# Layer 3 of a four-layer convolution kernel: q and k projections as single products under an account that carries room over, and the second head pair's scores first

## The chip, the cores and the metric

The kernel runs on one core of one Trainium2 chip. The metric is device time in microseconds. Three runs of the kernel before took 3479.43, 3482.70 and 3486.44 us, so its median is 3482.7 us. A profile of one further execution, which took 3485.36 us, is what the sections below read.

The engines are called as in the profile: PE is TensorE's matrix multiplier and PEld its weight load, DVE is VectorE, ACT is ScalarE, POOL is GpSimd, SP issues nearly all DMAs. Each engine runs its own instructions in the order in which the program gives them.

## The reference, cut to what matters

The input `x` has shape (4, 256, 48, 48). Four layers follow each other, each of the form `x = x + layer(_gn(x))` with a group norm over 32 groups. Layers 0 to 2 are convolutions; the change leaves them alone. Layer 3 is an attention without softmax, in three windows:

```python
q = jnp.einsum('bchw,oc->bohw', x, Wq).reshape(b * h, d, Hh, Ww)
k = jnp.einsum('bchw,oc->bohw', x, Wk).reshape(b * h, d, Hh, Ww)
v = jnp.einsum('bchw,oc->bohw', x, Wv).reshape(b * h, d, Hh, Ww)
q = jax.nn.sigmoid(q)
k = jax.nn.sigmoid(k)
v = v / jnp.maximum(jnp.linalg.norm(v, axis=1, keepdims=True), 1e-12)
...
for w in WINDOWS:                      # 1, 2, 4
    ws = Hh // w
    wk = _box(Ik, ws, Hh, Ww)          # sums of k over a window around each place
    wkv = _box(Ikv, ws, Hh, Ww)        # the same of k times v
    attn = jnp.einsum('bdhw,bdfhw->bfhw', q, wkv)
    norm = jnp.einsum('bdhw,bdhw->bhw', q, wk)
    attn = attn / (norm[:, None] + 1e-06)
    outs.append(attn.reshape(b, C, Hh, Ww))
o = jnp.concatenate(outs, axis=1)
return jnp.einsum('bchw,oc->bohw', o, Wout) + bout[None, :, None, None]
```

There are 8 heads of 32 channels. A window's sum of k times v, multiplied by q, is the same as the sum over the window's places of (q times k) times v, and this is how the kernel computes it.

## The kernel before, in words

**Blocks and steps of layer 3.** A block is one batch (4), one half of the channels (2, four heads each) and one block of 8 rows (6): 48 blocks in the list `order`. A block's keys come in tiles of 8 rows by 16 columns, `tiles_of` (line 2003): 12, 15 or 18 tiles for a block, near rows and far rows in turn. Each tile of each block is one step of the loop at line 2201; there are 720 steps, 180 for each batch, 90 for each half of the channels.

**What a step does.** It issues the scores of its tile (line 2206): for each of the two head pairs `pr` one PSUM tile `s` of two banks and two matmuls of 32 rows, which stand on different row groups of the array. `unseen` (line 1855) adds a large negative penalty with one matmul per head, pair 0 first. `masked` (line 1875) turns scores into masked sums `sm`. In a tile whose rows all lie in the widest window, ACT takes the edges of the second pair (`widest`) while DVE takes the middle window of the first pair (`middle`), and then ACT the edges of the first pair and DVE the middle of the second (lines 1943 to 1947). In a tile at row distance 3, ACT takes the first pair and DVE the second. In near tiles POOL multiplies the narrowest window's mask on. Two steps later (`LAG`, line 84) `sums` (line 1980) multiplies `sm` by the values into the three accumulators. The pool of `s` tiles has two buffers, so the next step's scores wait for this step's masks.

**The side jobs.** Everything else of layer 3 is a generator in the list `active`: the projections q, k, v of the next batch (`qk`, line 423; `v`, line 457), the window sums of k (`k_sums`, line 1621), the norms (`norms`, line 1663), the states (`state`, line 1761), the preparation of outputs (`prepare`, line 2017) and the output product (`finish`, line 2050). `advance` (line 302) runs once at the end of each step and lets each job go on to its next `yield`, in the order of the list: norms and `finish_all` were started first, so they come ahead of the projections of the next batch. A group of 8 rows gives eight projection jobs (a load, four of q and k, three of v), and `paced(following, 2)` starts one of them every two steps.

**The account.** The variable `spare` holds the nanoseconds of PE time that a step may give to side jobs. At the end of a step it becomes `min(spare, 0.0) + time` (line 306): a debt is carried on, room that was not used is dropped. `time` is `900.0 + mask_time - sums_time`, at least 500 (lines 2226 to 2229); `mask_time` (line 2170) prices the masks of this step, `sums_time` (line 2184) the sums that PE does in it. A job takes its turn with `turn(cost)` or `bank(steps, cost)` (lines 329 to 342), which wait until `spare` is at least 0.6 of its cost and then subtract the cost. `product_time` (line 349) prices a matmul at 1.67 ns a column, so one of 384 columns at 641 ns. An `advance()` without a time, as in `until` (line 318), grants `ALL`, which is without limit: that is how the loop forces a result that it needs at once, and how the first projections run beside the convolutions.

**The one bank.** `s` has four of the eight PSUM banks, the three accumulators have one each, and `ps_m` has the last one. All side products use it. `bank(steps, ...)` closes it for so many steps; with `HOLD` (1000) it is closed until `keep_bank(1)`. A q or k product is 256 channels deep, so it is two matmuls of 128 rows into the same tile; both are issued in one turn at a cost of 1,283 ns (line 430).

**The v chain.** After a group's third v product, POOL squares, DVE reduces, and POOL takes four steps of a Newton iteration for the reciprocal root (lines 500 to 505), one per step of the loop; a step later DVE multiplies `vt` by it (line 506). The norms of a block of rows put up to twelve operations of 128x384 on `nhi` to POOL within about four steps (lines 1705 to 1714).

## Time and profile before

| what | value |
|---|---|
| median of three runs | 3482.7 us |
| time of the profiled execution | 3485.36 us |
| its span, first to last instruction | 3483.6 us |
| first score of layer 3 | 1,389 us |
| busy in the span: PE, DVE, ACT, POOL | 3059.6, 1994.0, 1041.5, 1532.2 us |
| mean granted clock of TensorE | 0.951 |
| scores `s<-qs,ks` | 5760 records, mean 506 ns |
| sums `acc<-sm,vs` | 14976 records, mean 306 ns |
| q and k products in layer 3 | 148 and 148 records of a mean of 522 and 520 ns |
| wait of PE's scores for DVE and for ACT, layer 3 | 61.6 and 60.4 us |
| wait of PE's sums for POOL | 48.5 us |

A matmul in float32 leaves two records, so one q or k product leaves four. In a page of the profile, the slices cut the span into 40 equal parts of 87 us; each digit is the busy share in tenths. A row of the timeline gives start and length in us, engine, operation, what is written and read, and in brackets the idle time of the engine before it with what ended that. A row of the waits gives total, number and longest. The engine whose wait ends last in a step sets when the next step begins.

### The profile page before, as it was taken

The page shows a single profiled execution, that of the slowest core. Times are in us where ns is not written, and L with a number is a line of the kernel's source. Part 1 is how long each engine was busy: PE and PEld are TensorE (multiplying, and loading weights), DVE is VectorE, ACT ScalarE, POOL GpSimd, SP SyncE. Part 2 cuts the span into 40 slices and gives each one's busy share as a digit, 9 for nine tenths or more (in the row PEclk, how much of TensorE's full clock was granted, in tenths as well). Part 3 has the DMA queues.
Part 4 walks back from the last instruction along what each step waited for, and adds up shares of the span by engine and source line. Part 5 has one row for each costly group of instructions (what it writes and reads, how often), then busy time and mean ns, then how long its engine had stood idle before and what let it go on. Part 6 is the DMA issues. An engine that isn't in the chain of part 4 may idle for free.

```text
span 3483.6 us, 78045 instructions
## 1 busy us (share of the span) xinstructions
PE 3059.6 (88%) x31634; PEld 1931.6 (55%) x31634; DVE 1994.0 (57%) x3595; ACT 1041.5 (30%) x2782; POOL 1532.2 (44%) x2548
## 2 busy tenths in 40 slices
PE   3579999999899788888789988889998999989998
PEld 2467776767768557444344544444554444545544
DVE  7986488568657336465564445554456554444444
ACT  0012111211111423444323433433344433334432
POOL 0000030021011214587886678786557786534443
PEclk9799899999999899999899999999999999999999
DMA  7745413413322422344554444354423454401221
GB/s 256 236 139 174 141 63 122 154 54 129 120 94 85 138 89 98 120 132 145 164 144 129 127 137 146 116 158 134 124 81 119 130 150 122 114 29 52 81 63 56
DMA packets 373052, 423.34 MB, mean 122 GB/s; under 512 B 129076, under 2 KB 328532, under 8 KB 371540
## 3 DMA queue, kind: packets, MB, share of 16 engines
q1 hardware_dynamic: 371491, 416.32, 38.3%
q8 instruction: 249, 4.08, 0.5%
q0 software_dynamic: 144, 1.24, 0.2%
q14 instruction: 112, 0.91, 0.1%
q10 hardware_dynamic: 1056, 0.79, 0.1%
HBM read 288.24 MB, written 131.25 MB: 120 GB/s over the span
## 4 chain that ended last, share of the span: by engine, by line
PE 56%; POOL 12%; DVE 11%; ACT 4%; issue 3%; DMA 3%; SPq 1%; ACTq 0%; POOLq 0%; DVEq 0%
PE s L208 15%; PE cv L208 14%; PE acc L208 11%; PE out_ps L208 6%; PE proj_ps L208 4%; DVE sm L208 3%; POOL nhi L208 3%; ACT sm L208 3%; POOL sm L208 3%; POOL pt L208 2%; PE ap L208 2%; POOL vu L208 1%; DVE l2v L208 1%; DVE v L208 1%; DVE k L208 1%
## 5 line engine op out<-in xcount | busy, mean ns | idle before, releaser
L208 DVE TENSOR_TENSOR sm<-s,masks 128x432 f32<-128x432 f32 (+8 forms) x1152 | 634.4, 578 | 627.8 <-PE s L208 582.0
L208 POOL TENSOR_TENSOR sm<-sm,masks 128x336 f32<-128x336 f32 (+8 forms) x768 | 606.1, 809 | 662.6 <-DVE sm L208 656.2
L208 ACT ACTIVATE sm<-s 128x128 f32<-128x128 f32 (+3 forms) x1680 | 559.1, 361 | 1030.9 <-PE s L208 820.9
L208 PE MATMUL s<-qs,ks 32*128 32x320 f32 (+3 forms) x5760 | 664.5, 506 | 127.9 <-DVE sm L208 61.6
L208 PE MATMUL acc<-sm,vs 128*32 128x64 f32 (+13 forms) x14976 | 681.8, 306 | 48.6 <-POOL sm L208 48.5
L208 PE MATMUL cv<-vx,wt 128*128 128x288 f32 x2080 | 560.1, 425 | 93.2 <-DVE vx L208 52.6
L208 PEld LDWEIGHTS acc<-sm,vs 128*32 128x32 f32 x14976 | 347.9, 110 | 384.5 <-issue 258.4
L208 PEld LDWEIGHTS cv<-vx,wt 128*128 128x128 f32 x2080 | 402.5, 198 | 214.5 <-issue 56.7
L208 PEld LDWEIGHTS s<-qs,ks 32*128 32x128 f32 x5760 | 264.4, 187 | 422.9 <-ACT sm L208 172.4
L208 POOL MEMSET v<- 128x16 f32 (+1 forms) x120 | 18.5, 215 | 727.7 <-DVE vx L208 634.5
L208 PE MATMUL cv<-v,wl 128*128 128x384 f32 x1152 | 225.1, 355 | 25.7 <-DVE x L208 10.6
L208 DVE TENSOR_SCALAR sm<-s 128x672 f32<-128x672 f32 (+1 forms) x144 | 118.6, 824 | 202.8 <-PE s L208 198.1
L208 PEld LDWEIGHTS cv<-v,wl 128*128 128x128 f32 x1152 | 214.3, 194 | 36.0 <-issue 15.9
L208 PE MATMUL s<-masks 24*128 24x128 bf16 (+4 forms) x2880 | 217.7, 236 | 0.0
L208 POOL TENSOR_TENSOR pt<-pt 128x144 f32<-128x144 f32 x336 | 188.5, 561 | 23.0
L208 POOL TENSOR_TENSOR v<-l2v,v 128x384 fp32r<-128x384 f32 x96 | 109.0, 1163 | 120.2 <-ACT v L208 111.3
L208 POOL TENSOR_TENSOR nhi<-nhi,nq 128x384 f32<-128x384 f32 x144 | 144.8, 1033 | 0.2
L208 PE MATMUL cv<-pad,wl 128*128 128x384 bf16 x864 | 143.1, 327 | 0.0
L208 PE MATMUL out_ps<-o,wout_sb 128*128 128x384 f32 x288 | 130.2, 534 | 3.6 <-DVE res L208 2.8
L208 PEld LDWEIGHTS <-masks 24*128 24x128 bf16 x2880 | 101.5, 95 | 53.9 <-issue 3.5
L208 PEld LDWEIGHTS <-wl 128*128 128x128 bf16 x864 | 83.8, 97 | 59.3 <-issue 0.7
L208 PE MATMUL out_ps<-stage,wout_sb 128*128 128x384 f32 x288 | 116.4, 486 | 0.0
(176 smaller groups left out, 3568.6 us busy)
## 6 DMA issues: line engine op xcount, KB each, us to landing
wt<-wt SPq DMA_DIRECT2D x48, 768.0 KB
kb_d<-pt SPq DMA_DIRECT2D x48, 576.0 KB
rc<-r_d SPq DMA_DIRECT2D x192, 144.0 KB
nhi<-kb_d SPq DMA_DIRECT2D x120, 192.0 KB
nlo<-kb_d SPq DMA_DIRECT2D x88, 192.0 KB
o_d<-stage SPq DMA_DIRECT2D x24, 576.0 KB
o<-o_d SPq DMA_DIRECT2D x24, 576.0 KB
wl<-wl_d SPq DMA_DIRECT2D x16, 768.0 KB
```

Source lines behind the costliest of these rows:

```text
L208: return lambda *args, **kwargs: self.tc.keep_in_program_order(op(*args, **kwargs))
```

## The change

Four edits, all in the planning of layer 3:

1. The account carries unused room, up to `MOST` = 600 ns, and a step's room is `450.0 + mask_time - sums_time`, at least 300, in place of 900 and 500.
2. A q or k product takes its turn for each of its two matmuls at 641 ns. It holds the bank from the first one to the second, as `norms` and `finish` do.
3. `keep_bank(1)` opens the bank one step after the second matmul.
4. The scores of a step are issued for head pair 1 and then for pair 0. The list `ss` is turned back, so that penalties and masks come in the order of before.

```diff
-        spare = ALL if time is None else min(spare, 0.0) + time
+        spare = ALL if time is None else min(spare, MOST) + time
...
-    ALL = 1e6
+    ALL, MOST = 1e6, 600.0
...
             yield from take("kt")
-            yield from bank(1, NCT * product_time(NB))
+            yield from bank(HOLD, product_time(NB))
             ps = self.ps_tile()[:, 0:NB]
             for ct in range(NCT):
+                if ct > 0:
+                    yield from turn(product_time(NB))
                 pe.matmul(
...
+            keep_bank(1)
             self.used(g)
...
-                ss = [blocks[i].scores(pr, a, c) for pr in range(NPR)]
+                ss = [blocks[i].scores(pr, a, c) for pr in reversed(range(NPR))][::-1]
...
-                time = 900.0 + mask_time(*stream[n][:3]) - sums_time(*stream[n - LAG][:4])
-            advance(max(time, 500.0))
+                time = 450.0 + mask_time(*stream[n][:3]) - sums_time(*stream[n - LAG][:4])
+            advance(max(time, 300.0))
```

## The prediction

> **What bounds the kernel now.** I read the page first: its busy line, its slices, then the 87 us windows of layer 3, the waits, and two stretches of the timeline.

> ```profile
> PE 3059.6 (88%) x31634; PEld 1931.6 (55%) x31634; DVE 1994.0 (57%) x3595; ACT 1041.5 (30%) x2782; POOL 1532.2 (44%) x2548
> ...
> PE   3579999999899788888789988889998999989998
> ...
> POOL 0000030021011214587886678786557786534443
> PEclk9799899999999899999899999999999999999999
> ```

> Layer 3 runs from 1,389 us (slice 16) to the end: some 2,090 us, 720 steps. TensorE is its busiest engine, but POOL is close wherever projections and norms run. Three windows (us, then PE, PEld, DVE, ACT and POOL busy, granted clock, DMA):

> ```profile
> 1651.00:1738.00 87.00, 64.93 (x821) 34.19 (x819) 46.52 (x76) 28.57 (x84) 72.34 (x126) 0.85 0.59 176
> 1912.00:1999.00 87.00, 84.53 (x1145) 44.79 (x1141) 38.95 (x68) 35.57 (x105) 51.78 (x70) 1.00 0.42 124
> 3043.00:3130.00 87.00, 78.55 (x1236) 43.69 (x1234) 39.25 (x69) 30.82 (x93) 35.51 (x59) 1.00 0.09 29
> ```

> With POOL at 72 of 87 us, PE falls to 65 and the clock to 0.85; with POOL at 52, PE has 84.5 and the full clock. The waits of layer 3 (total, times, longest) say who holds whom:

> ```profile
> DVE vt L208 <- POOL vr L208: 104.7, 18, 12.1
> PE s L208 <- DVE sm L208: 61.6, 92, 9.5
> PE s L208 <- ACT sm L208: 60.4, 110, 4.0
> PE acc L208 <- POOL sm L208: 48.5, 36, 5.3
> ```

> The first is a jam. VectorE's scaling of v stands ahead of the next mask and waits for POOL's reciprocal roots, which stand behind the norms' `nhi` work:

> ```profile
> 1674.50 1.94 POOL L208 TENSOR_TENSOR nhi<-nhi,nlo 128x384 f32<-128x384 f32 x2
> 1678.26 1.09 PE L208 MATMUL acc<-sm,vs 128*32 128x132 f32 x6 [5.28 <-POOL sm L208]
> 1678.82 2.90 POOL L208 TENSOR_TENSOR nhi<-nhi,nq 128x384 f32<-128x384 f32 x3
> 1682.87 0.96 DVE L208 TENSOR_TENSOR vt<-vt,vr 128x768 f32<-128x768 f32 x1 [12.07 <-POOL vr L208]
> 1684.82 1.53 PE L208 MATMUL s<-qs,ks 32*128 32x320 f32 x8 [3.97 <-ACT sm L208]
> ```

> PE stands for 9 us; the scores then take 1.53 instead of 0.82 us, at half clock.

> I sorted the matmuls of layer 3 by step (from one step's first score to the next one's). 328 steps with no side product have a median of 2.07 us; 139 with about 0.54 us of them (at the account's prices) 2.56; 195 with about 1.28 us 3.26. Side work is thus almost additive: a step hides only some 0.1 to 0.4 us. Above 2.07 + 0.93 per us of side work, 42 long steps lose 170 us: 82 in batch 0, 51 in batch 1, 32 in batch 2, 5 in batch 3, which projects nothing. The half-clock stretches there (145 us, 72 us lost) are mostly inside that sum.

> [...] eight score records, 506 ns each on average, span 0.82 us[...]

> **The change part by part.**

> *Convolution stages.* The first q, k, v run there with unlimited room, so both halves of a product go in one turn: nothing moves before 1,389 us.

> *Room.* Evaluating mask time minus sums time for all steps gives a mean of 292 ns. Room is now max(900+d, 500), mean 1,223 ns, the unused part dropped; then max(450+d, 300), mean 793, with up to 600 carried. Demand per batch: 24 q/k at 1,283 ns, 18 v at 855, 24 state uses (12 states, a transpose and a product each) at 641, 12 norm turns and 36 output turns at 1,283: 123 us, 684 ns a step. Supply falls from 220 to 143 us: enough, but used to 86% instead of 56%.

> *q and k.* 74 products of layer 3 (296 records of four) are cut in two. No matmul is added. Split in two steps, each half finds its own slack: in steps of like d, 0.54 us of side work cost 0.37 where 1.28 cost 1.14, so a second step hides about 0.15 us more. With 1,393 at best after an idle step (600 + 793) both halves still go together (1,026 is needed), else not; I take 45 split: 45 x 0.15 = -7 us; bounds 0 and -30 (74 x 0.4). Behind a split move the sigmoid (490 ns on ACT), for k the copy (0.51), and two or one DMA issues (0.4 us each on SP), past the norms' loads in SP's order; their readers come steps later, which hides it; uncovered it is one step, 2 to 3 us, per product that somebody waits for.

> *The one bank.* q/k hold it about 1.6 steps instead of 1. Bank steps per batch, mine: q/k 24 to 38, v 18, states 24, norms 18 to 21, outputs 60 to 74 (a second-half turn finds 793 a step, not 1,223). Sum 144 to 175 of 180. Outputs and norms stand first in the list of jobs, projections last. Now q, k and v come in runs of ten steps in a row (steps 9 to 18 have 1.28 or 0.85 us in each), at over 1 us a step; with 0.79 a run of ten spreads over some fifteen.

> *Where the jam goes.* In batch 0 the norms run every 16 to 17 steps (copies at steps 57, 74, 91, 107) and the v chains too (scalings at 55, 71, 88, 103), since a group's eight jobs start two steps apart. A norm's `nhi` work (six products at 1.03 us and up to six differences at 0.97) thus falls on the four steps of the roots each time: near the worst phase. Later v's move off it, and one step of lag drains about 3 us of POOL's queue. A v chain late by 3 to 5 steps escapes most of a 9 us jam. But norms get about one step longer each and may meet other chains. I take a gain of a sixth of the 170 us: -28. Bounds: -80 (batch 0's jams gone) and +50 (batches 1 and 2 as bad as batch 0).

> *Second pair first.* Masks and penalties keep their order; only four matmuls swap. The timeline of two steps with no side work:

> ```profile
> 3161.12 0.93 PE L208 MATMUL s<-qs,ks 32*128 32x384 f32 x8 [0.43 <-DVE sm L208]
> 3162.13 1.52 DVE L208 TENSOR_TENSOR sm<-s,masks 128x624 f32<-128x624 f32 x2 [1.07 <-PE s L208]
> 3162.97 0.45 ACT L208 ACTIVATE sm<-s 128x128 f32<-128x128 f32 x2 [0.29 <-DVE sm L208]
> 3163.47 1.15 PE L208 MATMUL s<-qs,ks 32*128 32x384 f32 x8 [0.43 <-ACT sm L208]
> ```

> The first score waits once for VectorE, once for ACT: the first to be issued gets the buffer that comes free first. The other came 0.2 us later (1.15 instead of 0.93). Now that early start serves pair 0, whose penalty and first VectorE mask follow at once; swapped, it serves pair 1, whose penalty still stands behind pair 0's. Behind the waiting score on PE are the other pair, the penalties and the sums; VectorE waits for the first penalty. The spread between first and last penalty over 20 ns, my measure of that lead, sums to 35 us in all steps. Most is covered by sums or by ACT; I take +8 us; bounds -5 (ACT late, so its pair's lead helps) and +35.

> *Sum.* 3,485.4 us profiled (span 3,483.6 and 1.8 around it) - 7 - 28 + 8 = 3,458.4; the median of the runs stands 2.7 below: **3,456 us**.

> **The rivals.**

> *Nothing net (3,484 us: 3,482.7 - 7 + 8):* the jams only change places. For it: norms and v chains both stay near 16 to 18 steps, and POOL's work is the same. Against: the phase of batch 0 is nearly the worst.

> *The bank becomes the bound (3,508 us, slower).* At 175 of 180 steps the jobs that others wait for come late; the program then advances without scores until they are made. Step 8 shows the price: it waits for the states of the first window and takes 15.4 us, 12 over its like. Two such and +1 from the terms above: +25. It decides from where state transposes slip past the seventh step of their block; from batch 0's second half on they are loaded 30 steps or more ahead, which speaks against.

> *The swap costs its whole lead (3,500 us, slower):* +35 - 7, and a jam gain of only 10. For it: batch 3 has 129 steps with no side work of 179, and a gap of 0.2 us after most of its row-distance-3 steps. Against: the ACT chain, not VectorE, ends last in the light ones.

> That the change does not do what it says: carry is cut to 600 after every wait with unlimited room, so it can't run away; I give it nothing.

> **How the numbers follow.** Chances: gain 0.50 (3,456, own range 3,425 to 3,474), nothing net 0.18, bank 0.20, swap 0.12. What a measurement here tells from no change is 0.2%, 7 us. The gain is faster throughout; of nothing net 0.03 fall below 3,476 and 0.02 above 3,490; bank and swap are slower but for 0.01. Faster 0.53, same 0.14, slower 0.33. The range leaves out a tenth at each end: 3,425 to 3,511.

> **What would show it.** Right: VectorE's wait for `vr` well below 104.7 us; more steps with one q/k half and fewer without side work; POOL's busy share in the first half of batches 0 to 2 lower, in the second higher; the clock above 0.951; batch 3 (3,024 us to the end) 2 to 5 us longer. Wrong: long steps at block edges with PE waiting for states, or `vr` waits as large as before at other steps.

## Result and profile after

| six runs each | before | after |
|---|---|---|
| median | 3481.1 us | 3512.1 us |
| lowest to highest | 3472.4 to 3486.4 | 3499.7 to 3514.3 |
| time over before, with its 95% interval | | 1.0086 (1.0073 to 1.0100) |
| span of the profiled execution | 3483.6 | 3509.4 |
| mean granted clock of that execution | 0.951 | 0.945 |
| 719 step times of layer 3 | 2072.7 | 2104.3 |
| batches 0, 1, 2, 3 | 572.4, 546.3, 516.4, 437.7 | 582.6, 554.6, 525.7, 441.5 |

The kernel became 0.86% slower, 30 us where 27 us less were forecast. All of it lies in layer 3, eight to ten microseconds in each of the three batches that project the next one and four in the last. The page after: the same instructions, the same work on VectorE, ACT and POOL to within 2.2 us, but 25 us more of busy PE.

```profile
PE 3085.0 (88%) x31634; PEld 1934.3 (55%) x31634; DVE 1995.1 (57%) x3595; ACT 1043.7 (30%) x2782; POOL 1532.2 (44%) x2548
...
PE   3689999999899779889889998989999989999998
...
POOL 0000030020011214677885677776556786534443
PEclk9799899999999899989899999999999999999999
```

The three windows that answer those of before (us, then PE, PEld, DVE, ACT and POOL busy, granted clock, DMA):

```profile
1651.00:1738.00 87.00, 74.02 (x921) 37.75 (x913) 51.62 (x81) 32.85 (x95) 73.33 (x116) 0.91 0.60 182
1912.00:1999.00 87.00, 83.63 (x1131) 44.33 (x1127) 39.55 (x67) 34.93 (x100) 52.59 (x72) 1.00 0.44 130
3043.00:3130.00 87.00, 81.98 (x1206) 45.35 (x1202) 38.97 (x67) 34.96 (x108) 37.22 (x59) 1.00 0.11 36
```

The first one is even better than before (74 us of PE instead of 65, clock 0.91 instead of 0.85): the worst stretch was relieved. The loss is elsewhere. By halves of a batch (90 steps) the granted clock was 0.91, 0.95, 0.95, 0.99, 0.97, 0.97 in batches 0 to 2 before, and is 0.89, 0.94, 0.93, 0.97, 0.96, 0.98 after: a little lower nearly everywhere. The waits of layer 3 (total, times, longest):

```profile
DVE vt L208 <- POOL vr L208: 95.4, 18, 11.2
PE s L208 <- ACT sm L208: 60.1, 111, 4.0
PE s L208 <- DVE sm L208: 57.5, 83, 4.5
PE acc L208 <- POOL sm L208: 50.9, 43, 6.5
DVE ss L208 <- POOL sq L208: 14.7, 6, 6.1
ACT sg L208 <- DMA kf_d<-sg: 10.1, 1, 10.1
```

The four of before have hardly moved, 104.7 to 95.4 for v's roots at most. Of the two others, the reduction on VectorE that waits for POOL's squares stood at 6.4 us, and the sigmoid that waits for a store of k to empty its buffer did not occur in layer 3. (The sigmoids' wait for q's stores fell from 13.6 to 9.7.) No wait has grown by 30 us.

**The ledger of PE.** I merged PE's matmuls over layer 3 from the first score to PE's last matmul. Time without a matmul went from 193.7 to 200.1 us, +6.4. PE's busy time at half clock went from 111.4 to 147.8 us; I count half of the difference as lost, +18.2, an estimate from the granted clock of 0.50 there (eight scores of 32x320 in before took 1.53 us at 1684.82 with a granted clock of 0.50, and 0.82 us at 3152.16 with 1.00). What is left, PE's work put at full clock, went from 1840.7 to 1846.1, +5.4. The sum is +30.0. Counted by stretches that begin after the first score, with PE's idle time in them, half clock went from 144.9 us in 21 stretches to 181.2 us in 30; the prediction counts so, and so do the figures of half clock below. The granted clock of the six executions of after lies between 0.945 and 0.950, with a mean of 0.947; the one read here is at the low end. In these two executions, then, the change did not make PE wait much longer; **it made PE wait more often for about 2 us** (gaps of 1.5 to 2.5 us: 12 instead of 8), **and the larger part of the loss is half clock behind such waits.** The next two fences show how.

VectorE's scalings of v before, and what VectorE waited ahead of each (two of batch 0, three of batch 2):

```profile
1621.31 1.12 DVE L208 TENSOR_TENSOR vt<-vt,vr 128x768 f32<-128x768 f32 x1 [11.28 <-POOL vr L208]
1733.61 1.73 DVE L208 TENSOR_TENSOR vt<-vt,vr 128x768 f32<-128x768 f32 x1 [11.36 <-POOL vr L208]
2598.85 1.60 DVE L208 TENSOR_TENSOR vt<-vt,vr 128x768 f32<-128x768 f32 x1 [1.44 <-POOL vr L208]
2630.79 1.23 DVE L208 TENSOR_TENSOR vt<-vt,vr 128x768 f32<-128x768 f32 x1 [1.44 <-POOL vr L208]
2667.41 1.43 DVE L208 TENSOR_TENSOR vt<-vt,vr 128x768 f32<-128x768 f32 x1 [4.77 <-POOL vr L208]
```

The same scalings after:

```profile
1628.20 1.43 DVE L208 TENSOR_TENSOR vt<-vt,vr 128x768 f32<-128x768 f32 x1 [6.80 <-POOL vr L208]
1761.09 1.12 DVE L208 TENSOR_TENSOR vt<-vt,vr 128x768 f32<-128x768 f32 x1 [6.44 <-POOL vr L208]
2621.05 1.12 DVE L208 TENSOR_TENSOR vt<-vt,vr 128x768 f32<-128x768 f32 x1 [2.55 <-POOL vr L208]
2655.68 0.96 DVE L208 TENSOR_TENSOR vt<-vt,vr 128x768 f32<-128x768 f32 x1 [3.50 <-POOL vr L208]
2691.39 1.39 DVE L208 TENSOR_TENSOR vt<-vt,vr 128x768 f32<-128x768 f32 x1 [3.10 <-POOL vr L208]
```

The long waits of batch 0 became shorter, as forecast, and most of the short ones longer; in batch 1, not shown, the longest went from 9.39 to 11.24 us. Before, 12 of 18 scalings lay in or up to 8 us ahead of a half-clock stretch, after 15. These stretches hold 109.2 us in both kernels: nine microseconds less wait at the scalings bought nothing. The others doubled, from 7 stretches with 34 us to 14 with 68 (one more in each kernel begins behind PE's last matmul). After, six of these 14 begin behind sums that waited 1.4 to 3.1 us for POOL's masks, two behind VectorE's reduction waiting for POOL's squares, one behind a transpose of keys that waited 2.7 us for its load, one behind a sigmoid that waited for a store.

What a single such wait costs is seen around the scaling at 2655.68. Five windows of 3.41 us on the grid on which the clock changes (columns as above):

```profile
2650.85:2654.26 3.41, 2.33 (x40) 1.19 (x32) 1.32 (x2) 0.83 (x3) 3.02 (x9) 1.00 0.47 151
2654.26:2657.68 3.42, 1.59 (x12) 0.82 (x8) 2.00 (x3) 0.29 (x2) 1.38 (x6) 1.00 0.76 224
2657.68:2661.09 3.41, 3.21 (x21) 1.44 (x22) 2.12 (x4) 2.12 (x9) 3.25 (x5) 0.51 0.68 208
2661.09:2664.50 3.41, 3.41 (x17) 1.78 (x18) 0.00 (x0) 0.80 (x2) 1.26 (x3) 0.50 0.43 173
2664.50:2667.92 3.42, 3.42 (x50) 1.77 (x49) 2.23 (x3) 1.14 (x3) 2.63 (x4) 0.99 0.02 5
```

In the second window PE had work for 1.59 of 3.42 us. The next two are at half clock though PE is busy in them, 17 and 21 matmuls instead of some 50; by the same count 3.4 us of work are lost behind a wait of 3.5 us on VectorE. The scaling of before at 2630.79 waited 1.44 us, and PE stayed busy for 2.07 us of its window:

```profile
2630.76:2634.17 3.41, 2.07 (x20) 1.18 (x23) 2.89 (x5) 0.81 (x3) 3.11 (x5) 1.00 0.00 0
2634.17:2637.58 3.41, 3.41 (x48) 1.89 (x40) 2.77 (x5) 1.24 (x3) 3.30 (x6) 1.00 0.82 230
```

Nothing is lost there. Last, the two steps without side work, at the same place of batch 3:

```profile
3184.56 0.93 PE L208 MATMUL s<-qs,ks 32*128 32x384 f32 x8 [0.46 <-DVE sm L208]
3185.59 1.52 DVE L208 TENSOR_TENSOR sm<-s,masks 128x624 f32<-128x624 f32 x2 [1.08 <-PE s L208]
3186.43 0.45 ACT L208 ACTIVATE sm<-s 128x128 f32<-128x128 f32 x2 [0.30 <-DVE sm L208]
3186.93 1.15 PE L208 MATMUL s<-qs,ks 32*128 32x384 f32 x8 [0.44 <-ACT sm L208]
```

2.37 us from one step to the next, 2.35 before: these two steps show 0.02 us of cost for the swap.

### The profile page after: what moved, and what is told of

Its sections match the earlier page's. It is cut to its first block, busy times and chain, and to the rows that moved or that the text cites. A ratio compares the mean times of both kernels' runs of the same rounds, so it can differ in the third digit from the quotient of the medians.

```text
span 3509.4 us, 78068 instructions
## 1 busy us (share of the span) xinstructions
PE 3085.0 (88%) x31634; PEld 1934.3 (55%) x31634; DVE 1995.1 (57%) x3595; ACT 1043.7 (30%) x2782; POOL 1532.2 (44%) x2548
## 3 DMA queue, kind: packets, MB, share of 16 engines
q0 software_dynamic: 144, 1.24, 0.2%
## 4 chain that ended last, share of the span: by engine, by line
PE 54%; POOL 13%; DVE 11%; ACT 4%; issue 3%; DMA 3%; SPq 2%; ACTq 0%; POOLq 0%; DVEq 0%
PE s L208 15%; PE cv L208 14%; PE acc L208 11%; PE out_ps L208 5%; PE proj_ps L208 5%; POOL nhi L208 3%; POOL sm L208 3%; POOL pt L208 3%; DVE sm L208 3%; ACT sm L208 3%; PE ap L208 2%; SPq L208 2%; POOL vu L208 1%; DVE l2v L208 1%; DVE v L208 1%
## 5 line engine op out<-in xcount | busy, mean ns | idle before, releaser
L208 DVE TENSOR_TENSOR sm<-s,masks 128x432 f32<-128x432 f32 (+8 forms) x1152 | 634.9, 579 | 639.7 <-PE s L208 583.9
L208 POOL TENSOR_TENSOR sm<-sm,masks 128x336 f32<-128x336 f32 (+8 forms) x768 | 607.1, 811 | 693.7 <-DVE sm L208 691.8
L208 ACT ACTIVATE sm<-s 128x128 f32<-128x128 f32 (+3 forms) x1680 | 559.5, 362 | 1086.2 <-PE s L208 884.2
L208 PE MATMUL s<-qs,ks 32*128 32x320 f32 (+3 forms) x5760 | 668.7, 511 | 123.9 <-ACT sm L208 61.5
L208 PE MATMUL acc<-sm,vs 128*32 128x64 f32 (+13 forms) x14976 | 690.0, 308 | 51.5 <-POOL sm L208 50.9
L208 PE MATMUL cv<-vx,wt 128*128 128x288 f32 x2080 | 563.2, 427 | 89.4 <-DVE vx L208 49.0
L208 PEld LDWEIGHTS acc<-sm,vs 128*32 128x32 f32 x14976 | 350.4, 111 | 393.9 <-issue 262.4
L208 PEld LDWEIGHTS cv<-vx,wt 128*128 128x128 f32 x2080 | 404.5, 199 | 212.0 <-issue 52.7
L208 PEld LDWEIGHTS s<-qs,ks 32*128 32x128 f32 x5760 | 263.0, 189 | 429.3 <-ACT sm L208 169.8
L208 POOL MEMSET v<- 128x16 f32 (+1 forms) x120 | 18.5, 214 | 726.5 <-DVE vx L208 633.1
L208 PE MATMUL cv<-v,wl 128*128 128x384 f32 x1152 | 224.6, 354 | 24.8 <-DVE x L208 10.7
L208 DVE TENSOR_SCALAR sm<-s 128x672 f32<-128x672 f32 (+1 forms) x144 | 118.6, 824 | 223.0 <-PE s L208 199.1
L208 PEld LDWEIGHTS cv<-v,wl 128*128 128x128 f32 x1152 | 213.7, 194 | 35.1 <-issue 16.1
L208 PE MATMUL s<-masks 24*128 24x128 bf16 (+4 forms) x2880 | 215.1, 237 | 0.0
L208 POOL TENSOR_TENSOR pt<-pt 128x144 f32<-128x144 f32 x336 | 188.6, 561 | 23.0
L208 POOL TENSOR_TENSOR v<-l2v,v 128x384 fp32r<-128x384 f32 x96 | 109.0, 1163 | 118.6 <-ACT v L208 109.8
L208 PE MATMUL cv<-pad,wl 128*128 128x384 bf16 x864 | 143.2, 327 | 0.0
L208 POOL TENSOR_TENSOR nhi<-nhi,nq 128x384 f32<-128x384 f32 x144 | 142.1, 1014 | 0.2
L208 PE MATMUL out_ps<-o,wout_sb 128*128 128x384 f32 x288 | 131.6, 539 | 1.5 <-DVE res L208 1.4
L208 PEld LDWEIGHTS <-masks 24*128 24x128 bf16 x2880 | 101.4, 96 | 54.8 <-issue 5.5
L208 PE MATMUL out_ps<-stage,wout_sb 128*128 128x384 f32 x288 | 117.2, 489 | 2.3 <-DVE stage L208 2.3
L208 PEld LDWEIGHTS <-wl 128*128 128x128 bf16 x864 | 83.9, 97 | 59.5 <-issue 1.0
```

Source lines behind the costliest of these rows:

```text
L208: return lambda *args, **kwargs: self.tc.keep_in_program_order(op(*args, **kwargs))
```

## The experiments

All times are medians; the ratio is to the kernel before on the same chip, with its 95% interval. One percent is 35 us. The letters in the expectations: A says that the swap costs the lead of the first pair; B that the account and the split move side jobs, and that long steps, with waits behind POOL and the half clock after them, are the loss; C that the loss is in PE's own order under the smaller room.

### Each part alone

Without the swap, the diff against after:

```diff
-                ss = [blocks[i].scores(pr, a, c) for pr in reversed(range(NPR))][::-1]
+                ss = [blocks[i].scores(pr, a, c) for pr in range(NPR)]
```

> The changed kernel with the scores in the order of before (pair 0 first). Theory A (the swap takes away the first pair's lead; batch 3, with almost no side work, is 3.8 us longer in the changed kernel): about 4 us a batch come back, so some 3,497 us, +15 over before, and batch 3 back near 438 us. Theory B (the account and the split move side jobs so that long steps lose 202 us where they lost 170; the swap is free): 3,510 us, long steps still near 200 us.

Measured 3506.2 us, 1.0073 (1.0056 to 1.0090).

Before with the swap alone:

```diff
-                ss = [blocks[i].scores(pr, a, c) for pr in range(NPR)]
+                ss = [blocks[i].scores(pr, a, c) for pr in reversed(range(NPR))][::-1]
```

> The kernel before with the second pair's scores first and nothing else. Theory A: about 3,496 us, +15, spread evenly over the batches, batch 3 at 441 to 442 us. Theory B: 3,481 us, no change, long steps near 170 us.

Measured 3487.7 us, 1.0023 (1.0012 to 1.0033).

Before with the split of q and k alone:

```diff
-            yield from bank(1, NCT * product_time(NB))
+            yield from bank(HOLD, product_time(NB))
...
+                if ct > 0:
+                    yield from turn(product_time(NB))
...
+            keep_bank(1)
```

> The kernel before with q and k taken in two turns (bank held between them), room and carry as before. Theory A: 3,475 to 3,481 us, since at 1,223 ns of room a step both halves often go together. Theory B: nearly as before too, unless holding the bank alone does it; then 3,490 us or more and later norms.

Measured 3485.8 us, 1.0014 (1.0004 to 1.0024).

Before with the account alone:

```diff
-        spare = ALL if time is None else min(spare, 0.0) + time
+        spare = ALL if time is None else min(spare, MOST) + time
...
-    ALL = 1e6
+    ALL, MOST = 1e6, 600.0
...
-                time = 900.0 + mask_time(*stream[n][:3]) - sums_time(*stream[n - LAG][:4])
-            advance(max(time, 500.0))
+                time = 450.0 + mask_time(*stream[n][:3]) - sums_time(*stream[n - LAG][:4])
+            advance(max(time, 300.0))
```

> The kernel before with the new account (carry up to 600, 450 and 300 in place of 900 and 500), q and k products whole. Theory A: 3,481 to 3,488 us. Theory B: most of the loss is here: 3,500 to 3,510 us, long steps near 200 us, batch 3 unchanged at 438 us.

Measured 3499.4 us, 1.0056 (1.0039 to 1.0073). Half clock in layer 3 rose from 144.9 to 171.9 us, time without a matmul only from 193.7 to 196.0, and VectorE's wait for v's roots fell to 83.2 us.

**What follows.** The three parts add up: 0.23 + 0.14 + 0.56 is 0.93%, the whole 0.86%. The swap is a quarter of the loss, the split a seventh, the account most of it, with less of the wait that it was to shorten. A is out as the main cause: the swap costs 7 us where A had 15. B's range for the account, 3,500 to 3,510, is missed by less than one microsecond. B also left batch 3 at 438 us, and with the account alone it takes 441.3; with the swap alone it takes 440.4, so a longer batch 3 is no mark of the swap by itself.

### The carry or the smaller room

Before with the carry alone, the room left at 900 and 500:

```diff
-        spare = ALL if time is None else min(spare, 0.0) + time
+        spare = ALL if time is None else min(spare, MOST) + time
...
-    ALL = 1e6
+    ALL, MOST = 1e6, 600.0
```

> Before with the carry alone: min(spare, 600) in place of min(spare, 0); room stays 900 + d, at least 500. Theory B2 (the smaller room is what moves the v chains and spreads the jobs, the carry only pays part of it back): 3,470 to 3,482 us, within 5 us of before, since with the old room unused time was hardly needed. Rival C2 (the carry is what costs, since it lets a full output turn of 1.28 us into the step with the long sums): 3,486 to 3,495, most of the 19 us of the account.

Measured 3496.6 us, 1.0044 (1.0028 to 1.0061).

Before with the smaller room alone, the carry left at 0.0:

```diff
-                time = 900.0 + mask_time(*stream[n][:3]) - sums_time(*stream[n - LAG][:4])
-            advance(max(time, 500.0))
+                time = 450.0 + mask_time(*stream[n][:3]) - sums_time(*stream[n - LAG][:4])
+            advance(max(time, 300.0))
```

> Before with the smaller room alone: 450 + d, at least 300; unused room is dropped as before. Theory B2: 3,492 to 3,510, as much as the account as a whole (3,499) or more, with more half clock (over 165 us in layer 3; before 145) and v's scalings 3 to 10 steps later. Rival C2: 3,472 to 3,485.

Measured 3477.0 us, 0.9988 (0.9975 to 1.0001).

**What follows.** My theory (B2) had it upside down. The smaller room, which moves v's scalings most (in batch 1 from steps 212 to 281 to steps 225 to 311), costs nothing. The carry, with v's scalings nearly where they were (26, 39, 55, 71, 88, 102 in batch 0; before 26, 39, 55, 71, 88, 103), costs 16 us, 0.44%. The two make 0.32% where the account as a whole made 0.56%; the intervals leave open whether they add up. The ledger of PE in layer 3, one execution of each:

| us | without a matmul | of it in gaps over 4 us | PE busy at half clock |
|---|---|---|---|
| before | 193.7 | 38 (6 gaps) | 111.4 |
| carry alone | 207.3 | 69 (11) | 91.8 |
| smaller room alone | 188.0 | 52 (10) | 141.1 |
| account, both of them | 196.0 | 47 (9) | 139.2 |
| after | 200.1 | 42 (8) | 147.8 |

The carry's cost is thus not the clock. PE waits 13.6 us more, in long gaps, and works less at half clock than before; the granted clock of its six executions is 0.950 in the mean, as in the 18 of before that ran beside them. The smaller room has 30 us more at half clock, of which 15 are lost by the same count, and yet takes no longer: 5.7 us less without a matmul and 7.1 us less of work put at full clock make up for most of it. So more half clock does not always mean a slower kernel, and the clock's part in the whole change cannot be carried over to its parts. The rival's own reason, output turns in the step with the long sums, doesn't hold either: in the run with the carry alone these steps hold 40 us of side products instead of 18, and are only 3 us longer than that work explains. No single place holds the 16 us: lined up in tens of steps, the run loses 9 us at steps 250 to 259 and 8 at 430 to 439, and wins 6 back at 260 and 5 at 180. It has a kind of jam that before hardly has, here in step 102 (the timeline of SP, VectorE and PE in the run with the carry alone; start, length):

```profile
1716.82 7.11 SPq L208 DMA_DIRECT2D rc<-r_d  x4
1724.37 0.38 SPq L208 DMA_DIRECT2D kb_d<-pt  x1
1724.96 0.38 SPq L208 DMA_DIRECT2D kp<-kf_d  x1
1729.24 1.00 DVE L208 TENSOR_TENSOR_SCAN cs<-kp 128x304 f32<-128x304 f32 x1 [10.41 <-DMA kp<-kf_d]
1730.93 1.01 PE L208 MATMUL s<-qs,ks 32*128 32x384 f32 x2 [9.33 <-DVE sm L208]
```

The window sums of k load `kp`. The load stands on SP's queue behind the loads of `rc` for an output (four of the eight are shown) and a store of `pt`. These four took SP 7.1 us; the store and the load behind them were issued 0.6 us apart. The store's own data had been ready since 1712.2. VectorE's scan waits 10.4 us: the load is issued 6.1 us after VectorE fell idle and lands 4.2 us later. The next mask stands behind the scan and begins at 1730.17, though PE had its scores done by 1719.9, and PE waits 9.3 us for it. ACT's sigmoids wait 31.8 us for the stores of q (13.6 before) in this run. So a jam does not need v's chain: here a scan that reaches VectorE ahead of its data makes one.

### Is it the norms' work on POOL?

Before, and after, without the subtractions and the products by q in `norms` (this part of the norm is left out, `hi` goes on as it was loaded):

```diff
-                        pool.tensor_sub(hi[:, wi, n:RB], hi[:, wi, n:RB], lo[:, wi, n:RB])
...
-                    pool.tensor_mul(hi[:, wi], hi[:, wi], qf)
```

> The kernel before with POOL's differences and products of the norms left out (the box sums are taken as loaded; the outputs' divisors are thus others): 72 us of POOL work less per batch. Theory B: gaps of PE over 1.5 us fall from 25 to under 8, half-clock time under 50 us, about 3,370 us. Theory C: 3,460 to 3,481 us.

> The changed kernel with the same work left out. Theory B: 5 to 12 us over the before kernel with that work left out (what the swap costs), the account's part gone. Theory C: 25 to 30 us over it, as with the work.

Measured 3380.6 us, 0.9730 (0.9713 to 0.9747), and 3416.5 us, 0.9826 (0.9814 to 0.9839). The work is worth 96 us in the kernel before, where B had some 110, and VectorE's wait for v's roots falls to 49.5 us. But the change costs 36 us without it too. The roots' chain, with masks and output products on POOL, still makes VectorE wait for 56.1 us in the second kernel, and 12 of its 16 stretches of half clock have a scaling of v in them or up to 8 us ahead, eleven of these after a gap of PE of 1.9 to 4.3 us. B in its narrow form, v's chain behind the norms' work on POOL, is refuted: it had 5 to 12 us here.

The second kernel with v's scaling four steps later (the edit is that of the next experiment; as in the two runs above, all of the products are left out, not half of them as the expectation has it):

> After without the norms' differences and half of their products on GpSimd (part of the norms' computation is left out, as in the two runs before it), with v's scaling four steps later. In the run without the later scaling 12 of 16 half-clock stretches of layer 3 begin at a step with a scaling of v or right behind it, after a gap of 1.8 to 4.3 us. Theory B3 (the account's remaining cost is the reciprocal root's own chain on GpSimd with VectorE's masks behind it, also without the norms): those stretches go, half clock falls from 83 to below 50 us, time from 3,416 to 3,390 to 3,402. Rival C3 (the account's cost is in PE's own order and in the output turns): 3,408 to 3,418, the stretches move elsewhere.

Measured 3389.1 us, 0.9734 (0.9714 to 0.9755); half clock 61.6 us. The time is where B3 has it, a microsecond below; the half clock fell less than expected. The same run for the kernel before is missing, and with the norms' work in place the later scaling gains something in before too (next experiment), so how much of these 27 us was the change's own cost is not shown.

### The scaling of v out of the way

In `v`, between the last step of the Newton iteration and VectorE's product:

```diff
                 yield 1
+            yield 4
             dve.tensor_mul(
```

> The kernel before with VectorE's scaling of v four steps later than POOL's last root step, so that it no longer stands ahead of masks while POOL works off its queue. Theory B (jams behind POOL and the half clock after them are the loss): the wait of vt for vr falls from 105 us to under 20, half-clock time from 145 to under 90 us, and the time to about 3,430 us. Theory C (jams are only where an unavoidable wait shows; the loss of the change lies in PE's own order under the smaller room): within 10 us of 3,481.

> The changed kernel with the same later scaling. Theory B: most of its distance to the kernel before goes, since that is jams and clock: 8 to 15 us over the before kernel with the later scaling, so some 3,440 us. Theory C: still 30 us over it.

Measured 3461.1 us, 0.9960 (0.9944 to 0.9976), for before, and 3464.6 us, 0.9961 (0.9946 to 0.9976), for after. Four steps of delay take the wait for the roots away in both. After gains 1.25% by it, some 44 us, and before 0.40%, some 14: the two stand level. Half clock is 121.2 us in before and 107.9 in after. B is right that the distance between the kernels goes, but the times it named, 3,430 and 3,440, were not reached, nor its half clock under 90 us. Other waits have grown, ACT's for stores the most; in before with the later scaling:

```profile
ACT sg L208 <- DMA q_d<-sg: 29.0, 6, 10.3
ACT sg L208 <- DMA kf_d<-sg: 13.3, 3, 6.2
```

The first stood at 13.6 us, the second did not occur. That is the next experiment.

### The wait for the stores taken away too, and the change again

A third buffer for the sigmoid's output on top of it, for before, for after, and for after in the natural order of the pairs:

```diff
-            t = self.scr.tile([P, NB], F32, tag="sg", name="sg")
+            t = self.scr.tile([P, NB], F32, tag="sg", name="sg", bufs=3)
```

> Before with v's scaling four steps later and a third buffer for the sigmoid's output, so that ACT does not wait for the DMA that empties one (29.0 us, 6 waits, longest 10.3 in the run with the later scaling alone). If that wait stands on the path: 3,445 to 3,455 us, below the 3,461 of the later scaling alone, and a ratio to before of 0.992 to 0.994. If ACT's wait is covered, or another wait takes its place: 3,458 to 3,464, ratio 0.995 to 0.997.

> After with v's scaling four steps later and three buffers for the sigmoid's output. Theory W (the change's cost lies in side instructions that stand ahead of masks and wait for POOL or a DMA): with these waits gone it costs what the swap costs, so 3,444 to 3,454 us, ratio to before 0.988 to 0.991, 3 to 12 us above the same version of before. Theory A3 (the account has a cost of its own in PE's order): 3,462 to 3,475, ratio 0.994 to 0.997, 20 to 30 us above it.

> The same in the natural order of the pairs. Theory W: 3,434 to 3,446 us, ratio 0.986 to 0.990, equal to before with the two repairs. Theory A3: 3,455 to 3,470, ratio 0.992 to 0.997.

| with both repairs | us | ratio |
|---|---|---|
| before | 3441.1 | 0.9869 (0.9843 to 0.9894) |
| after | 3444.4 | 0.9898 (0.9878 to 0.9919) |
| after, natural order | 3436.9 | 0.9879 (0.9861 to 0.9897) |

The waits of the first row:

```profile
PE s L208 <- DVE sm L208: 39.6, 84, 3.0
PE s L208 <- ACT sm L208: 38.7, 96, 4.0
DVE cs L208 <- DMA kp<-kf_d: 10.0, 3, 5.4
ACT sg L208 <- DMA q_d<-sg: 1.6, 1, 1.6
```

And of the second row:

```profile
DVE ss L208 <- POOL sq L208: 24.2, 11, 8.4
DVE cs L208 <- DMA kp<-kf_d: 20.3, 4, 8.5
ACT sg L208 <- DMA q_d<-sg: 5.2, 2, 2.7
```

Theory W's times are met in both kernels of after. Where the waits for the roots and for the stores are gone or nearly so, account and split together cost 0.1% (-0.2 to +0.4% by the two intervals), where the same two cost 0.73% with the waits in place. The change still brings longer waits of VectorE's reduction (24.2 us; 0.5 in before with the repairs) and scan (20.3; 10.0), at a cost that cannot be told from nothing. The swap is left at 0.19%. The repair of before is better than forecast: the third buffer is worth another 0.9% on top of the later scaling. PE's waits for the masks, 122 us before, are 95 with the later scaling and 78 with both. This kernel is 39 us faster than the kernel before and some 70 faster than the kernel after.

### A pure shift

To see how far a mere shift moves the time, the projections of the next batch start 4, and 8, steps later, in the kernel before:

```diff
-                start(paced(following, 2))
+                active.append([step + 5, paced(following, 2)])
```

> Before, the projections of the next batch started 4 steps later, nothing else. Theory P (the phase of v chains against norms decides, so a pure shift moves the time by as much as the account does): a change of 8 to 25 us in either direction, with v's wait for its roots changed by over 15 us. Rival: within 5 us of before, since the same work is only done 8 us later.

> As the run with 4 steps, with 8: half a norm's period of 16 to 17 steps away, so the v chains of batch 0 should meet the norms in the other phase. Theory P: v's wait for its roots differs by over 20 us from 104.7, the time by 8 to 30 us, more likely down since batch 0 lies near the worst phase now. Rival: within 5 us of before.

Measured 3491.3 us, 1.0037 (1.0023 to 1.0052), and 3478.0 us, 0.9994 (0.9981 to 1.0008). The waits of the second:

```profile
DVE vt L208 <- POOL vr L208: 46.1, 16, 11.0
DVE ss L208 <- POOL sq L208: 29.8, 14, 5.2
DVE cs L208 <- DMA kp<-kf_d: 17.2, 3, 8.2
```

This is my forecast's own idea, the v chains moved half a period off the norms, and it does to that wait what I hoped of the change: -59 us. The median time stays. VectorE's reduction now waits 23 us more for POOL's squares, its scan of k 17 us for a load, and half clock has hardly moved (137.3 us against 144.9, with the stretch at the first score left out of both). This trace is of the slowest of 14 executions, 3487.8 us. With 4 steps the wait for the roots falls by 40 us (to 65.1) and the time rises by 13. For 4 steps theory P holds, for 8 its time is outside: a shift moves waits far, and the time by nothing to 13 us.

## Why the prediction was wrong

*Where the jam goes (-28 us): the step that failed.* It took a sixth of the 170 us lost in long steps as gained, because v's chains would come 3 to 5 steps later and leave the norms. They came 0 to 7 steps later in batch 0 (26, 39, 55, 71, 88, 103 became 31, 43, 55, 73, 91, 110) and VectorE's wait for them fell by 9 us. But the account by itself costs 19.5 us. The gain was to come from the smaller room, which makes v later, and that alone gives between -0.25 and +0.01%, at most 9 us; the carry, to which the prediction gave nothing, costs 16. The step took a shorter wait for the roots as time gained, and this is what fails. The time did not follow the wait: at 1621 us before, a wait of 11.3 us came with 10.2 us of half clock, at 2656 after, one of 3.5 us with 6.8, so spreading waits evenly gains little. The place was not free: the shift by 8 steps takes 59 us off the wait for the roots, the reduction then waits 23 us more for POOL's squares and the scan 17 us for loads, and the time stays. And jams have other sources, loads and stores, that move with the jobs. That such waits carry the account's cost is shown by the repairs, which take it away; which of them, and why the carry brings them, is not. The upper bound of +50 held the result.

*q and k split (-7 us, bounds 0 and -30): wrong in sign.* The work was split as said: 206 steps with about 0.57 us of side work instead of 139, 165 with 1.28 instead of 195, 289 with none instead of 328. In ordinary steps its price is as assumed: after, a step with about 0.57 us has a median of 2.62 us, 0.54 above an empty one, one with 1.28 us 3.33, 1.24 above, so two halves cost 0.16 us less than a whole. But the part alone measured +5 us, with 7 us more of half clock than before: what the ordinary steps save is lost elsewhere; where was not traced. The bounds left that out.

*Swap (+8 us): right.* 0.23% alone is 8 us; 0.13% and 0.19% on top of the rest are 5 and 7. The batch without projections took 3.8 us longer, where 2 to 5 were forecast; since the account alone lengthens it by 3.6, this does not speak for the swap alone.

*Sum.* Put in its terms: +5 for the split, +19.5 for the account, +8 for the swap, 32.5 instead of -27; measured 30.

*The rivals.* "Nothing net" had the cause nearest to it, jams that only change places, but let them do so at no cost. "The bank becomes the bound" named a time within 4 us of the measured one, but by luck: the one step where the program is driven on for want of a result and that grew, step 194, took 13.2 us instead of 9.8, which is 3 of the 25 us that this rival needs. The full loss of the swap's lead did not occur.

*What the profile was to show.* The wait for the roots is not well below 104.7 us. POOL's load moved from first halves to second ones in batch 0 only (225.4 and 202.8 us became 217.7 and 208.3), not in batch 1. The clock fell to 0.945 where above 0.951 was said; by the ledger that is 18 of the 30 us.

*What stays open.* Why the carry falls on bad places and the smaller room does not was not found; the trace of the run with the carry shows gains and losses of 4 to 9 us in turn. Which of the two repairs takes how much of the account's cost was not separated: the later scaling alone already brings before and after level, and the third buffer was not run alone. The later scaling also keeps `vt`, which has one buffer, four steps longer, so later v's of the same batch move too (in before to steps 32, 47, 62, 76, 92, 110); that its gain is the wait and not this move is likely, since the pure shifts gained nothing, but not shown. That the extra stretches of half clock cause the larger part of the loss is an account over two traces; no run changed the clock by itself, and the carry and the smaller room show that half clock and time can part.

## What to carry to other kernels

A side instruction on an engine that also does the main work can hold that work up: here VectorE's scaling of v waited 104.7 us in 18 waits with masks behind it, its scan of k in the run with the carry alone once 10.4 us, with PE's wait of 9.3 us behind that. Put such an instruction behind its data by some steps, or give it a buffer more, before tuning when its job starts. Two such edits gained 1.3% here and took away most of what this change of plan costs, while a better looking plan alone, by a change of account or a shift, gained nothing or cost up to 0.7%. And count TensorE's gaps of about 2 us (8 before, 12 after) beside the microseconds of a wait: neither number told the time alone.

## What was not expected of the hardware

| PE idle in the period | periods | next one at half clock |
|---|---|---|
| below 0.9 us | 1053 | 0 |
| 0.9 to 1.5 | 27 | 1 |
| 1.5 to 1.8 | 6 | 3 |
| 1.8 and more | 47 | 45 |

The idle time counted is the sum over the period: at 1412.2 us of before, half clock followed on 1.63 us of it in three gaps, the longest of 0.71 us. Of 98 periods at half clock, the next one ran at full clock after 51 of the 60 with less than 0.5 us of PE idle time, and after none of the 38 with more. These are counts over two traces of nearly the same kernel; no run set PE's idle time to a chosen length. Ahead of the prediction I took only long waits for dear ones. No trace showed that, and the periods with 1.8 us of idle time and more, 45 of 47 with half clock behind them, speak against it.
